# Softmax integers of a quantised cross-attention: two quarters of each row instead of one transposed by DMA, and one lag for all products with values

## The chip, the core and the metric

The kernel runs on one NeuronCore of a Trainium2 chip. The metric is the device time of one execution in microseconds (us). The core's engines each follow their own instruction queue: TensorE (PE in the profile; PEld is its weight load), VectorE (DVE), ScalarE (ACT), GpSimd (POOL) and SyncE (SP), which here only issues DMAs. All DMAs share 16 DMA engines.

## The reference, cut to what matters

The program is one layer of three parts on 512 query rows (4 x 128) of width 1024: a cross-attention to 8192 context rows, a causal self-attention, and a gated feed-forward with 4-bit weights. The change lies in the cross-attention alone:

```python
q = (x @ Wq + bq)...; k, v = (cond @ Wkv + bkv)...      # 16 heads of 64
q = _fq_sym(q, axis=-1); k = _fq_sym(k, axis=-1); v = _fq_sym(v, axis=2)
attn = softmax(einsum('bhqd,bhkd->bhqk', q, k))
attn = _fq_unsigned(attn, axis=-1)                       # round to 0..255
out = einsum('bhqk,bhkd->bhqd', attn, v)
```

Each softmax row has 8192 entries; rounded to integers 0 to 255 relative to its maximum, it is multiplied with the quantised values. TensorE contracts over partitions, so the integers, which come out with queries on partitions, must be transposed to have keys on partitions before that product.

## The kernel before, in words

Keys and values are first projected, quantised and written to DRAM (0 to about 1510 us). Then comes the attention stage (about 1513 to 2196 us), in which the change acts, then the output projection and the rest of the layer.

In the attention stage a **unit** is one head `h` and one tile `t` of 128 queries: 16 x 4 = 64 units. A unit has NSC = 8 **steps** `g` of SC = 1024 keys; four quarters `c` of KC = 2048 keys hold two steps each. A loop over `s` (line 882, inside a manual schedule, so that instructions stay on each engine in the order written) is a software pipeline:

- step `s` = 8n + g: `scores(n, g)`: two matmuls into the PSUM tile `sc` (2 buffers, line 761), then one custom VectorE instruction (line 768) that multiplies by the key scales, writes `e` (3 buffers, half a row each) and takes a running maximum `mx`. After g = 7 `maximum(n)` (lines 783, 785) makes the bias `m`.
- one unit later, at its steps 0 and 4: `exponentials` (line 796), the two halves of the row on ScalarE, written as int16 integers `a` (3 buffers).
- LAG_T = 12 steps after the scores: `transposes(n, g)` (lines 811 to 816): pairs of 16-bit integers are taken as one 32-bit word, four TensorE transposes of 128 x 128 words go to the PSUM tile `a_pt` (3 buffers), and one copy brings them to `aT` in SBUF (6 buffers). The copy is ScalarE's, but VectorE's for g = COPY_DVE = 4.
- quarter DMA_KC = 1 (g = 2 and 3) is transposed by one DMA from SyncE instead (`dma_transposes`, line 825), issued at step 4 of the next unit, into `aT_d` (2 buffers). TensorE's word transposes take even and odd keys apart and the DMA does not, so the order in which keys are stored depends on the quarter (`in_order`, line 571, used by `store_k` and `key_scales`).
- LAG_V = 16 steps after the scores (LAG_D = 20 for the quarter that the DMA transposes): `values(n, g)` (line 839): eight matmuls of 64 columns into the PSUM tile `av`, which holds the four units of a head and has one buffer. After the head's last product VectorE scales it into `xo` (lines 851 to 862).
- in a head's last unit (t = 3) SyncE loads the next head's keys `kt` (line 615, four DMAs) and GpSimd broadcasts its key scales (line 741); GpSimd's queue also loads the values `vq` (line 731, four DMAs for each pair of heads, 5 buffers) at given steps.

Of the kernel before, what the change touches and what calls it, by code (L numbers as in the profile page):

```python
# [36 lines left out]
F16 = mybir.dt.float16  # L37
I32 = mybir.dt.int32
# [8 lines left out]
P = 128  # L47
# [4 lines left out]
NP = H // 2  # L52
# [3 lines left out]
KC = 2048  # L56
NKC = NK // KC
SC = 1024
NSC = NK // SC
NEC = 2  # L60
EC = NK // NEC
LAG_T = NSC + 4
LAG_V = NSC + 8
COPY_DVE = 4
DMA_KC = 1
LAG_D = NSC + 12
INNER = 2816
WORDS = INNER // 8
V_AUTO = KT - 4
# [17 lines left out]
def tile_perceiver(  # L87
# [26 lines left out]
    nc = tc.nc  # L114
# [338 lines left out]
    for t, at in enumerate((4, 10.5, 20, 22.6)):  # L453
# [3 lines left out]
        for n in range(2):  # L457
            at = (10 + 8.15 * t, 42.6 + 7.05 * t)[n]
# [16 lines left out]
    at = 70.8  # L475
# [95 lines left out]
    def in_order(t, c):  # L571

        dims = "p h" if len(t.shape) == 3 else "p"
        if c == DMA_KC:
            return t.rearrange(f"{dims} (e n) -> {dims} n e", e=2)
        return t.rearrange(f"{dims} (n e) -> {dims} n e", e=2)

# [35 lines left out]
    def load_keys(h, c):  # L613
        kt = pools["keys"].tile([P, KC // 2], BF16, name=f"kt{h}_{c}", tag="kt", bufs=6)
        nc.sync.dma_start(out=kt, in_=k_d[c][h].rearrange("f d n -> (f d) n"))
        kts[h, c] = kt
# [5 lines left out]
    def load_scales(h, g):  # L622
        c, half = divmod(g, 2)
        nc.sync.dma_start(
            out=tile_of_scales(h, g), in_=sk_d[c][h, ts(half, SC)].partition_broadcast(P)
        )
# [4 lines left out]
    for s in range(V_AUTO, 2 * KT):  # L631
        at = TILE * s
# [8 lines left out]
    at = TILE * V_AUTO  # L641
# [11 lines left out]
    at = TILE * (KT - 2)  # L653
# [5 lines left out]
    at = TILE * KT  # L659
# [12 lines left out]
    for u in range(KT):  # L672
        at = TILE * (KT + u)
        s = KT + u
# [14 lines left out]
    at = TILE * (KT + 2)  # L689
# [4 lines left out]
    first, last = V_QUANT  # L694
    done = 0
    for u in range(first, last):
        at = TILE * (KT + u)
# [5 lines left out]
    at = TILE * (2 * KT - 1)  # L703
# [17 lines left out]
    with tc.tile_pool(name="at_s", bufs=4) as small, tc.tile_pool(  # L721
        name="at", bufs=2
    ) as at, tc.tile_pool(name="sc_ps", bufs=2, space=PSUM) as sc_ps, tc.tile_pool(
        name="at_ps", bufs=3, space=PSUM
# [3 lines left out]
        def load_values(p, c):  # L728

            vqs[p, c] = at.tile([P, KT // NKC, P], F16, name=f"vq{p}_{c}", tag="vq", bufs=NKC + 1)  # L730
            nc.gpsimd.dma_start(out=vqs[p, c], in_=vq_d[p, :, ts(c, KT // NKC), :])

        def load_rows(h):

            sks_at[h] = at.tile([P, KC], F32, name=f"sk_row{h}", tag="sk_row", bufs=1)
            for c in range(NKC):
                nc.gpsimd.dma_start(out=sks_at[h][32 * c : 32 * c + 1, :], in_=sk_d[c][h : h + 1, :])
# [7 lines left out]
        units = [(h, t) for h in range(H) for t in range(NT)]  # L745
        state, avs, sums = {}, {}, {}
# [44 lines left out]
        def exponentials(n, c):  # L791
            h, t = units[n]
            st = state[n]
            a = at.tile([P, EC], I16, name="a", tag="a", bufs=3)
            st["a"].append(a)
            nc.scalar.activation(  # L796
                a,
                st["e"][c],
                AF.Exp,
                bias=st["m"],  # L800
                scale=sq[:, t, h : h + 1],
                accum_out=sums[h][:, t, c : c + 1],
            )

        def transposes(n, g):

            a = state[n]["a"][g // (NSC // NEC)].bitcast(F32)
            at_word = SC // 2 * (g % (NSC // NEC))
            pt = at_ps.tile([P, SC // 256, P], F32, name="a_pt", tag="a_pt")
            for i in range(SC // 256):  # L810
                nc.tensor.transpose(  # L811
                    pt[:, i, :], a[:, at_word + P * i : at_word + P * i + P], ident
                )
            aT = at.tile([P, SC // 256, P], I32, name="aT", tag="aT", bufs=6)
            copy = nc.vector.tensor_copy if g == COPY_DVE else nc.scalar.copy
            copy(aT, pt.bitcast(I32))  # L816
            aT = aT.bitcast(F16).rearrange("p i (q e) -> p i e q", e=2)
            state[n]["aT", g] = [aT[:, i // 2, i % 2, :] for i in range(SC // P)]

        def dma_transposes(n):  # L820

            at_key = DMA_KC * KC % EC
            a = state[n]["a"][DMA_KC * KC // EC][:, at_key : at_key + KC].bitcast(F16)
            aT = at.tile([P, KC // P, P], F16, name="aT_d", tag="aT_d")
            nc.sync.dma_start_transpose(out=aT, in_=a)
            for g in range(KC // SC):
                state[n]["aT", KC // SC * DMA_KC + g] = [
                    aT[:, g * (SC // P) + i, :] for i in range(SC // P)
                ]

        def values(n, g):
            h, t = units[n]
            p, j = divmod(h, 2)
            if t == 0 and g == 0:
                avs[h] = at_ps.tile([P, NT, D], F32, name="av", tag="av", bufs=1)
            last = g == KC // SC * (DMA_KC + 1) - 1
            for i, aT in enumerate(state[n].pop(("aT", g))):
                c, k = divmod(g * (SC // P) + i, KT // NKC)
                nc.tensor.matmul(  # L839
                    avs[h][:, t, :],  # L840
                    lhsT=aT,
                    rhs=vqs[p, c][:, k, ts(j, D)],
                    start=(g == 0 and i == 0),
                    stop=(last and i == SC // P - 1),
                )
            if not last:
                return
            del state[n]
            if t == NT - 1:
                r = small.tile([P, NT], F32, name="r", tag="r")  # L850
                nc.vector.tensor_reduce(r, sums[h], AX.X, ALU.add)
                nc.vector.reciprocal(r, r)
                o = xo[h // 8][:, :, ts(h % 8, D)]
                nc.vector.scalar_tensor_tensor(  # L854
                    o,
                    avs[h],
                    F16_UNITS,
                    sv[:, ts(h, D)].unsqueeze(1).to_broadcast([P, NT, D]),
                    ALU.mult,
                    ALU.mult,  # L860
                )
                nc.vector.tensor_tensor(
                    o, o, r.unsqueeze(2).to_broadcast([P, NT, D]), ALU.mult
                )
# [2 lines left out]
        load_keys(0, NKC - 1)  # L867
        for g in range(NSC - 2, NSC):
            load_scales(0, g)

        order = [c for c in range(NKC) if c != DMA_KC] + [DMA_KC]
        load_rows(1)
        nc.sync.dma_start(out=sv, in_=sv_d[0].partition_broadcast(P))
        nc.sync.dma_start(out=bp, in_=xbp.partition_broadcast(P))
# [1 line left out]
        n_steps = len(units) * NSC  # L876

        def at_step(s):
            return divmod(s, NSC) if 0 <= s < n_steps else None

        with tc.manual_schedule():
            for s in range(n_steps + LAG_D):
                n, g = divmod(s, NSC)
                if s == 1:
                    for c in order:
                        load_values(0, c)
                if g == NSC // NEC and 1 <= n <= len(units):
                    dma_transposes(n - 1)
                if g % (NSC // NEC) == 0 and 1 <= n <= len(units):
                    exponentials(n - 1, g // (NSC // NEC))  # L890
                if n < len(units):
                    h, t = units[n]
                    scores(n, g)
                    if t == NT - 1 and h + 1 < H:

                        if g < NKC:
                            load_keys(h + 1, g)
                        spread_scales(h + 1, g)
                        if g == NSC - 1 and h + 2 < H:
                            load_rows(h + 2)  # L900
                    if g == NSC - 1:
                        maximum(n)
                for lag, work, dma in (
                    (LAG_T, transposes, False),
                    (LAG_V, values, False),
                    (LAG_D, values, True),
                ):
                    at_lag = at_step(s - lag)
                    if at_lag and (at_lag[1] * SC // KC == DMA_KC) == dma:
                        work(*at_lag)  # L910

                pair, since = divmod(s - NSC * (2 * NT - 1), NSC * 2 * NT)
                if 0 <= pair < NP - 1 and since in (0, LAG_V + 1, LAG_V + 5, LAG_V + 7):
                    load_values(pair + 1, order[(0, LAG_V + 1, LAG_V + 5, LAG_V + 7).index(since)])


    xq.close()
# [287 lines left out]
    with tc.manual_schedule():  # L1205
# [11 lines left out]
        for h, (w, n) in enumerate(PARTS):  # L1217
            s = PART * h

            if h > 0:  # L1220
                for kp in range(NC // 2):
                    at = s + {1: (-28, -22, -16, -10), 2: (-37, -33, -6, -3)}.get(h, (-26, -16, -6, -3))[kp]
# [15 lines left out]
            for t in range(NT):  # L1238
                g = s + GROUP * t
# [42 lines left out]
        s = PART * len(PARTS)  # L1282
        for i in range(2):
            at = s - 26 + 10 * i
# [9 lines left out]
    with tc.tile_pool(name="ff_t", bufs=2) as ff_t, tc.tile_pool(name="ff", bufs=1) as ff:  # L1294
# [63 lines left out]
        with tc.tile_pool(name="ff_h", bufs=1) as ff_h, tc.tile_pool(  # L1358
            name="y_ps", bufs=1, space=PSUM
        ) as y_ps:  # L1360
            y = ff_h.tile([P, NT, C], F32, name="y")
            for n in range(2):
# [4 lines left out]
                for q in range(NI // 2):  # L1367
# [5 lines left out]
                    for t in range(NT):  # L1373
                        for j in (2 * q, 2 * q + 1):
                            for i, ps in enumerate((yab[t][0], yab[t][0], yab[t][1])):
# [5 lines left out]
                                    stop=(j == NI - 1 and i != 0),  # L1381
# [91 lines left out]
```

## Time and profile before

| | |
|---|---|
| median of 3 runs | 2919.16 us (2917.12 to 2919.83) |
| the profiled execution, its own time | 2917.71 us |
| its span, first to last instruction | 2915.9 us |
| granted TensorE clock over the span | 0.985 |
| PE busy over the span | 2714.9 us (93%) |
| DVE busy | 2447.8 us (84%) |
| ACT busy | 1308.2 us (45%) |
| line 768 on DVE (512 instructions) | 595.1 us, first at 1513.4, last at 2181.1 us |
| line 796 on ACT (128) | 487.4 us |
| line 816 on ACT (320) and on DVE (64) | 168.4 us; 682 to 691 ns each on DVE |

Shares over the whole span mix stages: TensorE fills the projection before and much of the layer behind, so the attention stage must be read by itself. In the profile, "busy" adds up instructions of an engine, "idle before" is the engine's wait, and the name behind the arrow is what ended the wait. Two instructions that follow each other on an engine overlap a little in the records, so the cost of one in a row is best read as the distance between two starts.

### The profile page before, as it was taken

Reading aid. Unit: us, or ns where it says so; the run is one execution under the profiler, and the core shown is the slowest. Engines: PE = TensorE matmul, PEld = TensorE weight load, DVE = VectorE, ACT = ScalarE, POOL = GpSimd, SP = SyncE. Lnnn points to the kernel's source line nnn. Section 1 sums busy time; section 2 is a strip of 40 time slices with the busy share of each in tenths; the row PEclk is TensorE's granted clock in tenths of the full one; section 3 lists DMA queues with packets and bytes.
Section 4 is the critical chain, followed back from the end, with each engine's and each line's share of the span. In section 5 each row is a group of like instructions: output and inputs, shape, how many; then the busy total and the mean of one; then the engine's idle time right before and its main releaser. Section 6 shows DMA issues by size and latency. Waiting matters only on the chain.

```text
span 2915.9 us, 42024 instructions
## 1 busy us (share of the span) xinstructions
PE 2714.9 (93%) x15992; PEld 2103.4 (72%) x15992; DVE 2447.8 (84%) x4010; ACT 1308.2 (45%) x1473; POOL 442.0 (15%) x596
## 2 busy tenths in 40 slices
PE   8999999999999999999978888888878899799998
PEld 3788888888888888888845555555555677688876
DVE  6899998555799888989769999999995898676674
ACT  4212121111323333333229999999994244333332
POOL 0011111000022222222113223322311000000000
PEclk9999999999999999999979999999999999899999
DMA  5555565222457777776354445444433221122222
GB/s 184 179 199 195 197 214 196 99 89 101 145 132 199 195 183 195 185 189 177 98 164 90 104 94 108 109 107 99 95 81 128 87 77 58 51 94 94 94 87 94
DMA packets 321226, 383.83 MB, mean 132 GB/s; under 512 B 224064, under 2 KB 228736, under 8 KB 321024
## 3 DMA queue, kind: packets, MB, share of 16 engines
q1 hardware_dynamic: 274528, 227.02, 28.9%
q0 software_dynamic: 45440, 153.09, 16.3%
q8 instruction: 125, 2.05, 0.3%
q10 hardware_dynamic: 1056, 1.05, 0.2%
q14 instruction: 77, 0.63, 0.1%
HBM read 224.30 MB, written 104.34 MB: 113 GB/s over the span
## 4 chain that ended last, share of the span: by engine, by line
PE 69%; DVE 16%; issue 8%; ACT 5%; DMA 1%; POOL 0%; SPq 0%; DVEq 0%; ACTq 0%; POOLq 0%
PE kv_a L344 32%; PE kv_b L344 16%; DVE e L768 10%; PE y_a L1376 3%; PE gate_a L165 3%; PE up_a L165 3%; PE acc_a L1031 3%; ACT aT L816 2%; ACT a L796 2%; PE q_ps L293 2%; PE y_b L1376 1%; PE gate_b L165 1%; PE up_b L165 1%; PE acc_b L1031 1%; PE a_pt L811 1%
## 5 line engine op out<-in xcount | busy, mean ns | idle before, releaser
L344 PE MATMUL kv_a<-w_h,c_h 128*128 128x512 f32 x2048 | 806.4, 394 | 0.0
L344 PE MATMUL kv_a<-w_l,c_l 128*128 128x512 f32 x2048 | 806.0, 394 | 0.2 <-ACT w_l L247 0.2
L344 PE MATMUL kv_b<-w_d,c_d 128*128 128x512 f32 x2048 | 805.9, 394 | 0.0
L768 DVE CUSTOM_DVE_ANT_0 e<-sc,sk 128x1024 f32<-128x1024 f32 x512 | 595.1, 1218 | 13.1 <-DMA kt<-k_d 11.4
L796 ACT ACTIVATE a<-e,m,sq 128x4096 int16<-128x4096 f32 x128 | 487.4, 3808 | 19.4 <-DVE m L785 14.2
L344 PEld LDWEIGHTS kv_a<-w_l,c_l 128*128 128x128 f32 x2048 | 384.8, 188 | 89.6 <-ACT w_l L247 0.6
L344 PEld LDWEIGHTS kv_a<-w_h,c_h 128*128 128x128 f32 x2048 | 384.8, 188 | 88.9 <-issue 0.2
L344 PEld LDWEIGHTS kv_b<-w_d,c_d 128*128 128x128 f32 x2048 | 384.8, 188 | 88.9 <-DVE c_d L159 0.2
L155 ACT ACTIVATE c_h<-c_raw 128x1024 fp32r<-128x1024 f32 x128 | 135.1, 1056 | 422.5 <-PE kv_a L344 412.7
L358 DVE SCALAR_TENSOR_TENSOR f<-kv_a,bkv 128x512 f32<-128x512 f32 x256 | 175.6, 686 | 164.3 <-PE kv_a L344 163.6
L761 PE MATMUL sc<-kt,qT 64*128 64x512 bf16 x1024 | 204.0, 390 | 107.2 <-DVE mx L768 98.7
L811 PE MATMUL a_pt<-ident,a 128*128 128x128 f32 x1536 | 253.9, 288 | 13.0 <-ACT a L796 7.9
L811 PEld LDWEIGHTS a_pt<-ident,a 128*128 128x128 f32 x1536 | 162.6, 142 | 104.2 <-issue 49.7
L583 ACT CAST kst<-kT 128x512 bf16<-128x512 int16 x128 | 94.5, 738 | 301.2 <-DMA kT<-ki 301.1
L741 POOL PARTITION_BROADCAST sk<-sk_row x120 | 143.2, 1297 | 332.7 <-DVE mx L768 332.3
L359 DVE SCALAR_TENSOR_TENSOR f<-kv_b,f 128x512 f32<-128x512 f32 x256 | 176.6, 690 | 20.0 <-DVE f L358 1.4
L761 PEld LDWEIGHTS <-qT 64*128 64x128 bf16 x1024 | 76.6, 93 | 148.8 <-issue 106.7
L816 ACT COPY aT<-a_pt 128x512 int32<-128x512 int32 x320 | 168.4, 586 | 3.8 <-PE a_pt L811 3.6
L158 DVE TENSOR_TENSOR fw_l<-fw_raw,fw_h 128x1024 fp32r<-128x1024 f32 x64 | 78.2, 1223 | 107.1 <-ACT fw_h L155 107.0
L839 PE MATMUL av<-vq,aT 128*128 128x64 f16 x3072 | 154.3, 194 | 14.4 <-DVE xo L854 14.4
L839 PEld LDWEIGHTS <-aT 128*128 128x128 f16 x3072 | 130.2, 99 | 49.0 <-issue 43.8
L158 DVE TENSOR_TENSOR c_l<-c_raw,c_h 128x1024 fp32r<-128x1024 f32 x128 | 155.6, 1216 | 4.9 <-ACT c_h L155 4.1
(190 smaller groups left out, 3998.1 us busy)
## 6 DMA issues: line engine op xcount, KB each, us to landing
c_raw<-in_ctxT SPq DMA_DIRECT2D x128, 512.0 KB, 3.8
v_d<-f POOLq DMA_DIRECT2D x64, 512.0 KB, 3.1
vl<-v_d POOLq DMA_DIRECT2D x64, 512.0 KB, 4.2
gu_d<-w_ffn POOLq DMA_DIRECT2D x44, 512.0 KB, 3.1
fw_raw<-gu_d SPq DMA_DIRECT2D x42, 512.0 KB, 3.2
k_d<-kst POOLq DMA_DIRECT2D x128, 128.0 KB, 3.5
vq_d<-vq POOLq DMA_DIRECT2D x32, 512.0 KB, 4.9
kt<-k_d SPq DMA_DIRECT2D x64, 256.0 KB, 3.3
```

What stands on the lines that cost most here:

```text
L158: nc.vector.tensor_tensor(lo, src, hi, ALU.subtract)
L165: nc.tensor.matmul(ps, lhsT=lhs(i, k), rhs=rhs(i, k), start=(k == 0 and i != 1), stop=(k == NC - 1 and i != 0),)
L344: nc.tensor.matmul(ps, lhsT=tokens[s][i][:, k, :], rhs=w3[s < KT][k][i][:, ts(n, 512)], start=(k == 0 and i != 1), stop=(k == NC - 1 and i ...
L358: nc.vector.scalar_tensor_tensor(f, a, 1.0 + 1.0 / UP, bias[s < KT][n], ALU.mult, ALU.add)
L359: nc.vector.scalar_tensor_tensor(f, b, -1.0 / UP, f, ALU.mult, ALU.add)
L741: nc.gpsimd.partition_broadcast(tile_of_scales(h, g), sks_at[h][32 * c : 32 * c + 1, ts(half, SC)], channels=P)
L761: nc.tensor.matmul(ps[:, ts(i, 512)], lhsT=qT[rows, h, ts(t, P)], rhs=kts[h, g // 2][rows, ts(g % 2, 512)], start=True, stop=True,)
L768: nc.vector.tensor_tensor_reduce(out=state[n]["e"][-1][:, ts(g % (NSC // NEC), SC)], in0=ps, in1=sks_at[h, g], scale=1.0, scalar=LOWEST, o ...
L796: nc.scalar.activation(a, st["e"][c], AF.Exp, bias=st["m"], scale=sq[:, t, h : h + 1], accum_out=sums[h][:, t, c : c + 1],)
L811: nc.tensor.transpose(pt[:, i, :], a[:, at_word + P * i : at_word + P * i + P], ident)
L816: copy(aT, pt.bitcast(I32))
L839: nc.tensor.matmul(avs[h][:, t, :], lhsT=aT, rhs=vqs[p, c][:, k, ts(j, D)], start=(g == 0 and i == 0), stop=(last and i == SC // P - 1),)
```

## The change

A second quarter, c = 3 (g = 6 and 7), is transposed by DMA, issued at step 0 of the unit after the next. TensorE then transposes g = 0, 1, 4 and 5 only, and all their copies are ScalarE's. All products with values follow 18 steps behind the scores. `aT` has 4 buffers, `aT_d` 3. The keys of quarter 3 are stored in the order of the DMA's quarters. Values are loaded in natural order, at other steps.

```diff
-LAG_V = NSC + 8
-COPY_DVE = 4
-DMA_KC = 1
-LAG_D = NSC + 12
+LAG_V = NSC + 10
+DMA_KC = (1, 3)
...
-        if c == DMA_KC:
+        if c in DMA_KC:
...
-            aT = at.tile([P, SC // 256, P], I32, name="aT", tag="aT", bufs=6)
-            copy = nc.vector.tensor_copy if g == COPY_DVE else nc.scalar.copy
-            copy(aT, pt.bitcast(I32))
+            aT = at.tile([P, SC // 256, P], I32, name="aT", tag="aT", bufs=4)
+            nc.scalar.copy(aT, pt.bitcast(I32))
...
-        def dma_transposes(n):
+        def dma_transposes(n, c):
...
-            aT = at.tile([P, KC // P, P], F16, name="aT_d", tag="aT_d")
+            aT = at.tile([P, KC // P, P], F16, name="aT_d", tag="aT_d", bufs=3)
             nc.sync.dma_start_transpose(out=aT, in_=a)
...
-            last = g == KC // SC * (DMA_KC + 1) - 1
...
-                    stop=(last and i == SC // P - 1),
+                    stop=(g == NSC - 1 and i == SC // P - 1),
...
-            if not last:
+            if g < NSC - 1:
...
-                    for c in order:
+                    for c in range(NKC):
                         load_values(0, c)
                 if g == NSC // NEC and 1 <= n <= len(units):
-                    dma_transposes(n - 1)
+                    dma_transposes(n - 1, DMA_KC[0])
+                if g == 0 and 2 <= n <= len(units) + 1:
+                    dma_transposes(n - 2, DMA_KC[1])
...
-                for lag, work, dma in (
-                    (LAG_T, transposes, False),
-                    (LAG_V, values, False),
-                    (LAG_D, values, True),
-                ):
-                    at_lag = at_step(s - lag)
-                    if at_lag and (at_lag[1] * SC // KC == DMA_KC) == dma:
-                        work(*at_lag)
+                at_lag = at_step(s - LAG_T)
+                if at_lag and at_lag[1] * SC // KC not in DMA_KC:
+                    transposes(*at_lag)
+                if at_step(s - LAG_V):
+                    values(*at_step(s - LAG_V))
...
-                if 0 <= pair < NP - 1 and since in (0, LAG_V + 1, LAG_V + 5, LAG_V + 7):
-                    load_values(pair + 1, order[(0, LAG_V + 1, LAG_V + 5, LAG_V + 7).index(since)])
+                if 0 <= pair < NP - 1 and since in (0, LAG_V + 1, LAG_V + 3, LAG_V + 5):
+                    load_values(pair + 1, max(0, since - LAG_V + 1) // 2)
```

More of the change, by code (lines that the diff above doesn't have):

```diff
@@ L813, in transposes @@
                 )
-            aT = at.tile([P, SC // 256, P], I32, name="aT", tag="aT", bufs=6)
-            copy = nc.vector.tensor_copy if g == COPY_DVE else nc.scalar.copy
-            copy(aT, pt.bitcast(I32))
+            aT = at.tile([P, SC // 256, P], I32, name="aT", tag="aT", bufs=4)
+            nc.scalar.copy(aT, pt.bitcast(I32))
             aT = aT.bitcast(F16).rearrange("p i (q e) -> p i e q", e=2)
             state[n]["aT", g] = [aT[:, i // 2, i % 2, :] for i in range(SC // P)]
-        def dma_transposes(n):
-            at_key = DMA_KC * KC % EC
-            a = state[n]["a"][DMA_KC * KC // EC][:, at_key : at_key + KC].bitcast(F16)
-            aT = at.tile([P, KC // P, P], F16, name="aT_d", tag="aT_d")
+        def dma_transposes(n, c):
+            at_key = c * KC % EC
+            a = state[n]["a"][c * KC // EC][:, at_key : at_key + KC].bitcast(F16)
+            aT = at.tile([P, KC // P, P], F16, name="aT_d", tag="aT_d", bufs=3)
             nc.sync.dma_start_transpose(out=aT, in_=a)
             for g in range(KC // SC):
-                state[n]["aT", KC // SC * DMA_KC + g] = [
+                state[n]["aT", KC // SC * c + g] = [
                     aT[:, g * (SC // P) + i, :] for i in range(SC // P)
@@ L869, in tile_perceiver @@
             load_scales(0, g)
-        order = [c for c in range(NKC) if c != DMA_KC] + [DMA_KC]
         load_rows(1)
@@ L881, in tile_perceiver @@
         with tc.manual_schedule():
-            for s in range(n_steps + LAG_D):
+            for s in range(n_steps + LAG_V):
                 n, g = divmod(s, NSC)
                 if s == 1:
-                    for c in order:
+                    for c in range(NKC):
                         load_values(0, c)
                 if g == NSC // NEC and 1 <= n <= len(units):
-                    dma_transposes(n - 1)
+                    dma_transposes(n - 1, DMA_KC[0])
+                if g == 0 and 2 <= n <= len(units) + 1:
+                    dma_transposes(n - 2, DMA_KC[1])
                 if g % (NSC // NEC) == 0 and 1 <= n <= len(units):
```

## Prediction, made before the changed kernel ran

> **What bounds the kernel now.** The page gives PE 93% of the span and DVE 84%, but the change acts only while line 768 runs, so I first read the busy time of each engine in stretches of that stage (columns: PE, weight loads, DVE, ACT, POOL busy, clock, DMA share, GB/s).
>
> ```profile
> 1700.00:1800.00 100.00, 81.94 (x975) 57.97 (x976) 99.09 (x195) 96.07 (x86) 27.92 (x31) 1.00 0.47 108
> 1800.00:1900.00 100.00, 83.50 (x1016) 59.02 (x1015) 99.16 (x192) 97.05 (x88) 34.08 (x39) 1.00 0.46 99
> 1900.00:2000.00 100.00, 82.05 (x973) 57.85 (x972) 99.16 (x192) 96.88 (x87) 25.00 (x28) 1.00 0.42 93
> ```
>
> Here VectorE is the bound (99% busy), ScalarE is close (97%), PE has 17% and DMA more than half to spare. Next, the timeline of one unit, for what VectorE's period is made of and how far ScalarE is from it (columns: start, duration, engine, line, operation; in brackets idle time).
>
> ```profile
> 1806.04 1.22 DVE L768 CUSTOM_DVE_ANT_0 e<-sc,sk 128x1024 f32<-128x1024 f32 x1
> 1806.14 3.80 ACT L796 ACTIVATE a<-e,m,sq 128x4096 int16<-128x4096 f32 x1
> ...
> 1807.19 0.69 DVE L816 COPY aT<-a_pt 128x512 int32<-128x512 int32 x1
> ...
> 1807.80 1.21 DVE L768 CUSTOM_DVE_ANT_0 e<-sc,sk 128x1024 f32<-128x1024 f32 x1
> ...
> 1808.94 1.22 DVE L768 CUSTOM_DVE_ANT_0 e<-sc,sk 128x1024 f32<-128x1024 f32 x1
> ...
> 1809.95 1.54 ACT L816 COPY aT<-a_pt 128x512 int32<-128x512 int32 x3
> ...
> 1811.37 3.82 ACT L796 ACTIVATE a<-e,m,sq 128x4096 int16<-128x4096 f32 x1
> ...
> 1815.16 1.07 ACT L816 COPY aT<-a_pt 128x512 int32<-128x512 int32 x2
> ...
> 1816.12 0.21 DVE L785 TENSOR_SCALAR m<-m,nsq 128x1 f32<-128x1 f32 x1
> ...
> 1816.25 1.21 DVE L768 CUSTOM_DVE_ANT_0 e<-sc,sk 128x1024 f32<-128x1024 f32 x1
> ...
> 1816.36 3.80 ACT L796 ACTIVATE a<-e,m,sq 128x4096 int16<-128x4096 f32 x1
> ```
>
> The period is 1816.25 - 1806.04 = 10.21 us: eight line-768 instructions about 1.145 us apart (9.16), a copy, and the maximum (0.45). With the copy between them two line-768 starts are 1.76 us apart here, 1.74 in the next unit: the copy costs **0.60 us**. ScalarE: exponential to copies 3.81 and 3.79 us, three copies to the next exponential 1.42, two copies about 0.95 (they end at 1816.23, and the other exponential overlapped its copies by 0.12), so a copy costs 0.47 and the unit needs 9.97 us; for the rest it waits for `m`. Last, the DMA transposes, by their tile (issue on SyncE in ns, min/median/max, then issue to landing):
>
> ```profile
> L825 SPq DMA_TRANSPOSE aT_d<-a x64: 1665/1983/3858, 1528.5 to 2186.7; - x64
> ...
> DMA to landing us min/median/max: 4.2/4.4/6.9
> ```
>
> **The change, part by part.**
>
> *VectorE's copy goes.* 64 copies; those of the last two units start at 2182.68 and 2192.68, behind the last line-768 instruction (2181.09), so 62 lie on the bounding engine: 62 x 0.60 = **-37.2 us**. The unit becomes 9.61 us.
>
> *What is late next: ScalarE.* It makes five copies now (g = 0, 1, 5, 6, 7) and four after, two behind each exponential: 2 x (3.80 + 0.95) = 9.50 us, 0.11 under VectorE. Cost 0, with little cover. Above: priced by their full 586 ns, four copies and two exponentials of 3.80 make 9.94, and the gain shrinks to 0.27 us a unit (rival B). Below: nothing, since VectorE is behind it. VectorE's step 4 reuses the `e` buffer that the first exponential frees: that ends about 4.0 us into the unit, step 4 begins at 4 x 1.145 = 4.58, so 0.5 us cover.
>
> *TensorE* loses two of six groups of four transposes a unit (0.66 us busy each). It is not the bound: 0 gain. Its copies are due no sooner: products move from 16 to 18 steps for g = 0, 1, 4 to 7, which is 2.3 us more room; for g = 2, 3 from 20 to 18. The copies of g = 0, 1 end at the unit's end and are read two steps later. Four `aT` buffers fit four tiles a unit, read six steps after their transposes and rewritten after eight. Cost 0.
>
> *A second DMA transpose a unit.* In the trace it is seen at quarter-microsecond resolution, with nothing beside it, from about 1821.4 to 1824.2 us: a DMA share of 0.9 to 1.2, in all 2.9 us of the 16 engines for 512 KB. Four units take 41.85 us (first scale broadcasts of two heads, 1839.00 and 1880.85), so 10.46 a unit on average, of which DMA is busy 0.455 x 10.46 = 4.8 us. After: 7.7 of about 9.9 us, 77%: it fits. Waits on SyncE: the transpose of quarter 1 waits for the first exponential (4.0 us into the unit), that of quarter 3 for the second (about 8.7 us, a microsecond before the step at which it is written), so they alternate 4.7 and 4.9 us apart, each about 2 us of issue. Behind them queue the next head's four `kt` loads, held back by up to 2 us of issue, with 9 us until their first use and 3.4 us to land. Deadlines of the transposes: products eight steps after the step of issue, at least 9.2 us; and the exponential that rewrites the source buffer, one unit and about a microsecond after the issue. Landing takes 4.4 us, at worst 6.9. Cost 0; what is queued behind a late one is ScalarE's exponential, and behind that VectorE (rival C). Of the three `aT_d` buffers each is free about three steps before its next use.
>
> [...]
>
> *Values' loads* move to steps 19, 21, 23 and are needed at 28, 30, 32: 10 us for 3.8 (at worst 6.8) to land. GpSimd waits longer for `av`, with no broadcast behind it until step 32. *Key order of quarter 3*: its ScalarE casts (line 583) take 0.62 instead of 0.78 us, as quarter 1's do; ScalarE waited 301 us for its transposes there. Both 0.
>
> *Scaling of a head's output* (lines 851 to 862) moves from behind the maximum to behind step 1. It delays line 768 by 1.04 us now; then PE has finished the last product about 1 us earlier, so no wait; the extra gap in the row of line-768 instructions costs 0 to 0.1 us, taken 0.1 x 15 = **+1.5 us**. PE's next product waits for it until about 3.2 us into the unit, its scores for step 3 are ready at 3.9 and used at 4.5.
>
> *The end of the stage.* Before: bias ready at 2182.76, first scaling of the last head at 2195.95, 13.2 us. After: first exponential +3.9, two copies instead of three, second exponential done at about +8.7, then the DMA transpose of quarter 3, 4.4 to land (bounds 4.2 and 6.9), and 16 products, 0.8: about 14.0. **+0.8 us** (bounds 0.6 and 3.3).
>
> Sum: -37.2 + 1.5 + 0.8 = -34.9 us. The profiled execution's 2917.7 us (span 2915.9 and 1.8 around it) becomes 2882.8; the median of the runs is 1.5 us above it: **2884 us**.
>
> **The rivals.**
>
> *A, the forecast*, 0.68. VectorE stays the bound. From 2876 (the two costs vanish, and VectorE's remaining idle time of 0.85% of 668 us mostly with them) to 2892 (the tail at 3.3, ScalarE's bound 0.1 us higher a unit).
>
> *B, ScalarE becomes the bound*, 0.12. By the full durations above: 62 x 0.27 = 17 us less gain on top of the two costs: about 2905. For it: 97% busy, 0.11 us of cover. Against it: the starts, which give 0.47 a copy in both groups.
>
> *C, slower: transfers on SyncE's queue do not overlap.* 0.12. If each kept the queue from issue to landing, a head would need 8 x 4.4 + 4 x 3.4 = 48.8 us, against 39.5 that VectorE will need and 41.85 now: +7 x 16 = 111 us, 3030 us. It decides once a head's transfers exceed 39.5 us. For it: all go through one queue, and no two of these transposes were in flight together before. Against it: the engine time is 2.9 us of the 4.4, and a `kt` of 256 KB lands in 3.4 us though the engines moved up to 397 GB/s then.
>
> *D, slower: TensorE's clock falls*, 0.03. The first units' score matmuls take 0.61 us a pair (0.39 later) with idle gaps of 0.53, so a half-busy PE stayed slow. PE is busy 83% of 10.46 = 8.7 us a unit now and (8.7 - 1.3) / 9.9 = 75% after, at full speed. [...] By the row, slow scores and transposes (1.11 us) and products 1.6 times as long (0.61 by 0.39; 0.64 us for eight, an estimate) make 8 x 0.61 + 4 x 1.11 + 8 x 0.64 = 14.4 us a unit: +270 us, about 3190. I take 0: the loss of work is small.
>
> *E, the gain is given back* by a wait between B and C, 0.05: about 2919.
>
> **How the numbers follow.** This kernel's measurement can tell about 0.2% (5.8 us) from no change. Faster: A + B = 0.80; same: E, 0.05; slower: C + D, 0.15. The range reaches from A's lower end over B and half of E to 2920 and leaves out C, D and a little else. A's own range is 2876 to 2892.
>
> **What would show it.** Right: line 816 only on ACT, 256 times; starts of line 768 even at 1.145 us, unit 9.6; DVE still near 99% in the stage; last line-768 start about 36 us earlier (near 2145); DMA share near 0.77; PE near 75% at clock 1.0. Wrong: idle time before line 768 ended by ACT (B), exponentials that wait for a DMA and landings over 9 us (C), score pairs at 0.61 us inside the stage (D), a tail over 17 us.

## The result, and the profile after

| | before | after |
|---|---|---|
| median (4 runs each) | 2918.14 us | 2889.50 us |
| range | 2916.08 to 2919.83 | 2888.83 to 2893.55 |
| profiled execution, its own time / span | 2917.71 / 2915.9 us | 2888.83 / 2887.1 us |
| first and last start of the score instruction on DVE | 1513.4, 2181.1 us | 1510.9, 2149.3 us |

The ratio is 0.9905 with a 95% interval of 0.9888 to 0.9922: 28.6 us faster by the medians, where 2884 us (34 to 35 us) was forecast. Lines 768, 796, 811, 816 and 839 of the kernel before are 766, 794, 809, 813 and 835 now.

The same three stretches of the attention stage (columns as before: PE, weight loads, DVE, ACT, POOL busy, granted clock, DMA share, GB/s):

```profile
1700.00:1800.00 100.00, 78.78 (x970) 55.20 (x970) 98.39 (x189) 95.91 (x81) 36.26 (x40) 0.98 0.83 160
1800.00:1900.00 100.00, 78.07 (x960) 54.76 (x960) 98.39 (x195) 97.72 (x84) 24.89 (x28) 0.98 0.77 149
1900.00:2000.00 100.00, 79.51 (x960) 56.06 (x960) 97.48 (x189) 94.18 (x77) 36.94 (x41) 0.97 0.82 165
```

DMA has risen to about 0.81 as expected (0.77), VectorE is still the bound. But two columns are not as forecast: VectorE fell from 99.1 to 98.1, and TensorE's clock from 1.00 to 0.98. One unit in the timeline:

```profile
1801.60 1.21 DVE L766 CUSTOM_DVE_ANT_0 e<-sc,sk 128x1024 f32<-128x1024 f32 x1
1801.72 3.80 ACT L794 ACTIVATE a<-e,m,sq 128x4096 int16<-128x4096 f32 x1
...
1802.74 1.22 DVE L766 CUSTOM_DVE_ANT_0 e<-sc,sk 128x1024 f32<-128x1024 f32 x1
...
1803.88 1.22 DVE L766 CUSTOM_DVE_ANT_0 e<-sc,sk 128x1024 f32<-128x1024 f32 x1
...
1805.52 1.05 ACT L813 COPY aT<-a_pt 128x512 int32<-128x512 int32 x2
...
1806.46 3.81 ACT L794 ACTIVATE a<-e,m,sq 128x4096 int16<-128x4096 f32 x1
...
1810.26 1.06 ACT L813 COPY aT<-a_pt 128x512 int32<-128x512 int32 x2
...
1811.19 1.21 DVE L766 CUSTOM_DVE_ANT_0 e<-sc,sk 128x1024 f32<-128x1024 f32 x1
```

The unit is 1811.19 - 1801.60 = 9.59 us, the score instructions are even at 1.14 us, and ScalarE has two copies behind each exponential: the main step of the prediction as written. A unit in which VectorE also scales a finished head is longer; the others are called plain here. The 64 units, from the first start of each to the next: 9.59 to 9.62 us for nearly all plain ones (10.19 to 10.21 before), and 10.65 us for nine of the fifteen that hold a head's scaling (11.24 before). The rest stand out: after the first three units, six units with a scaling last 11.38 to 11.58 us, and two plain ones 10.71 and 10.72. In one of the six, what happens is seen in the clock (three stretches of 5 us, then TensorE and VectorE around the middle one):

```profile
1770.00:1775.00 5.00, 3.48 (x46) 2.64 (x47) 4.86 (x13) 5.00 (x5) 0.00 (x0) 1.00 1.16 307
1775.00:1780.00 5.00, 4.57 (x40) 3.09 (x39) 4.23 (x9) 5.00 (x6) 0.00 (x0) 0.66 0.81 164
1780.00:1785.00 5.00, 3.89 (x50) 2.75 (x48) 4.93 (x11) 3.03 (x3) 1.30 (x2) 1.00 0.82 186
```

```profile
1773.82 0.39 PE L835 MATMUL av<-vq,aT 128*128 128x64 f16 x8 [1.35 <-DVE xo L850]
...
1776.42 0.64 PE L835 MATMUL av<-vq,aT_d 128*128 128x64 f16 x8
1776.98 0.61 PE L759 MATMUL sc<-kt,qT 64*128 64x512 bf16 x2
1777.52 1.11 PE L809 MATMUL a_pt<-ident,a 128*128 128x128 f32 x4
1778.43 0.63 PE L835 MATMUL av<-vq,aT_d 128*128 128x64 f16 x8
1779.00 0.60 PE L759 MATMUL sc<-kt,qT 64*128 64x512 bf16 x2
```

```profile
1777.63 1.23 DVE L766 CUSTOM_DVE_ANT_0 e<-sc,sk 128x1024 f32<-128x1024 f32 x1
...
1779.64 1.22 DVE L766 CUSTOM_DVE_ANT_0 e<-sc,sk 128x1024 f32<-128x1024 f32 x1 [0.77 <-PE sc L759]
```

For about 3.4 us TensorE runs at half clock (0.50 granted from 1776.05 to 1779.46 us): scores 0.61 instead of 0.39 us, transposes 1.11 instead of 0.66. A step with transposes then takes about 2 us (score starts 1776.98 and 1779.00), VectorE runs out of scores and waits. In the whole stage VectorE's idle time before the score instruction, ended by scores from TensorE, went from 0.8 to 6.9 us (us, times; the kernel before, then the changed one):

```profile
  PE sc L761: 0.8, 2
...
  PE sc L759: 6.9, 13
```

A stretch of some 3.4 us at half clock like this one is called a dip below. Between 1540 and 2145 us the changed kernel has eight; the kernel before had one, at 2037 us, which lengthened no unit.

The DMA transposes, by their tile:

```profile
L822 SPq DMA_TRANSPOSE aT_d<-a x128: 1678/1944/4958, 1526.0 to 2159.7; - x128
...
DMA to landing us min/median/max: 4.2/4.3/9.0
```

Twice as many, the median issue and landing much as before, only the worst cases longer.

### The profile page after: what moved, and what is told of

The parts are those of the page before. It is cut to its first block, busy times and chain, and to the rows that moved or that the text cites. A ratio compares the mean times of both kernels' runs of the same rounds, so it can differ in the third digit from the quotient of the medians.

```text
span 2887.1 us, 41022 instructions
## 1 busy us (share of the span) xinstructions
PE 2666.1 (92%) x15480; PEld 2066.9 (72%) x15480; DVE 2411.5 (84%) x3946; ACT 1271.2 (44%) x1409; POOL 444.4 (15%) x596
## 3 DMA queue, kind: packets, MB, share of 16 engines
q10 hardware_dynamic: 1056, 1.05, 0.2%
## 5 line engine op out<-in xcount | busy, mean ns | idle before, releaser
L809 PE MATMUL a_pt<-ident,a 128*128 128x128 f32 x1024 | 176.9, 298 | 22.7 <-ACT a L794 18.0
L809 PEld LDWEIGHTS a_pt<-ident,a 128*128 128x128 f32 x1024 | 112.9, 146 | 88.6 <-ACT a L794 50.6
L157 DVE SCALAR_TENSOR_TENSOR c_d<-c_l,c_raw 128x1024 fp32r<-128x1024 f32 x128 | 156.3, 1221 | 2.3
L153 ACT ACTIVATE fw_h<-fw_raw 128x1024 fp32r<-128x1024 f32 x64 | 67.7, 1060 | 179.5 <-PE y_a L1369 75.2
L548 ACT CAST vq<-vi 128x1024 f16<-128x1024 int16 x64 | 66.9, 1046 | 172.2 <-DVE vi L541 123.8
```

The source lines that it names most:

```text
L153: nc.scalar.mul(hi, src, 1.0 - 0.5 / UP)
L157: nc.vector.scalar_tensor_tensor(df, lo, -1.0 - UP, src, ALU.mult, ALU.add)
L809: nc.tensor.transpose(pt[:, i, :], a[:, at_word + P * i : at_word + P * i + P], ident)
```

## The experiments

Theory 1: the missing part of the gain is these clock dips, set off by TensorE's wait (1.35 us above) for a head's scaling. Theory 2: TensorE's lighter load itself sets them off. Theory 3: the DMA engines, 80% busy, make something late. "Idle behind scores" below is VectorE's, over the stage; dips are counted between 1540 and 2145 us.

**e1: two product tiles**, so that TensorE need not wait for the scaling.

```diff
-            pt = at_ps.tile([P, SC // 256, P], F32, name="a_pt", tag="a_pt")
+            pt = at_ps.tile([P, SC // 256, P], F32, name="a_pt", tag="a_pt", bufs=2)
-                avs[h] = at_ps.tile([P, NT, D], F32, name="av", tag="av", bufs=1)
+                avs[h] = at_ps.tile([P, NT, D], F32, name="av", tag="av", bufs=2)
```

> The changed kernel with two buffers for the product tile of a head (and, to make room in PSUM, two instead of three for the transposes), so that TensorE no longer waits about 1.35 us for the scaling of the head before. Theory 1 (the missing 6 us of the gain are stretches of about 3.5 us in which TensorE's clock is halved, set off by that wait among light steps): no clock dips inside the stage, idle time of line 766 behind scores falls from 6.9 us to about 1.2 us (that of the first steps), about 5.5 us faster than the changed kernel, 2884 us. Theory 2 (the dips come from TensorE's lower load as a whole): the dips stay, within 1.5 us of 2889.5. Theory 3 (the 80% busy DMA engines make something late): within 1.5 us as well, with the waits still there.

**e2: the control**, the first of the two edits alone.

> The control for the run before: the changed kernel with two instead of three buffers for the transposes alone. TensorE can then wait for ScalarE's copies once a unit. All theories: VectorE has about 0.5 us of cover, so within 3 us of 2889.5, with the clock dips still there; if it is faster by 5 us, the buffers and not the wait for the scaling explain the run before.

Measured: e1 2906.2 us (ratio to before 0.995, 0.9934 to 0.9967), e2 2903.8 us (0.9951, 0.9936 to 0.9965). They are some 17 and 14 us slower than the changed kernel, so e2's own expectation failed: two buffers for the transposes are not free. TensorE's transposes wait for ScalarE's copies, and most plain units become 9.67 to 9.78 us:

```profile
PEld a_pt L809 <- ACT aT L813: 53.6, 65, 1.0
...
PE a_pt L809 <- ACT aT L813: 34.3, 57, 0.7
```

(e2, waits between 1700 and 2100 us: total us, times, longest; the changed kernel has 14.0 us of the first between 1690 and 2080 and the second not at all.) For the question at hand the pair is still of use: with the wait for the scaling (e2) there are fourteen dips and idle behind scores is 14.9 us, without it (e1) twelve and 13.3 us, in a profile that caught e1's fastest run. Removing the wait brought no time. Theory 1 in this form falls: while VectorE scales for a microsecond it takes no scores, and in e1 TensorE's longest wait for it to free a score buffer is 1.5 us instead of 0.5, so TensorE is short of work anyway.

**e3: more work for TensorE.** The scores of steps 2 and 3, in which it has no transposes, are done twice; the result is the same.

```diff
-            for i in range(2):
+            for i in (0, 1, 0, 1) if g in (2, 3) else (0, 1):
```

> The changed kernel, in which the two score matmuls of steps 2 and 3 of every unit are done twice (same result, 128 x 2 matmul pairs more, about 0.33 us of TensorE each), in the very steps that are light. Theories 1 and 2 (clock): more work on TensorE, yet fewer or no dips, about 4 to 6 us faster than the changed kernel, 2884 us. Theory 3 (DMA): no gain; the scores take 0.33 us more where they are late, so 0 to 3 us slower.

Measured: 2883.6 us (2880.4 to 2884.8), ratio 0.9877 (0.9862 to 0.9892). It does more, moves the same bytes, and is faster by about 6 us than the changed kernel, whose four runs lie at 2888.8 to 2893.6. In the profiles, first to last score instruction takes 633.2 us instead of 638.4. Two dips are left; thirteen of the fifteen units with a scaling last 10.64 to 10.66 us, and idle behind scores is 2.6 us. A stretch without a dip (the first below; the second has one) has the clock and VectorE's 99% back, at nearly the same DMA share:

```profile
1700.00:1800.00 100.00, 82.24 (x1018) 55.20 (x1015) 99.12 (x193) 96.83 (x84) 36.20 (x40) 1.00 0.80 160
1800.00:1900.00 100.00, 82.61 (x1009) 55.56 (x1007) 98.35 (x193) 96.32 (x81) 24.85 (x28) 0.98 0.78 150
```

So the clock is the cause; theory 3 does not explain a gain from extra matmuls.

**e4: the lag alone** on the kernel before (one quarter by DMA, the copy still on VectorE).

```diff
-LAG_V = NSC + 8
-LAG_D = NSC + 12
+LAG_V = NSC + 10
+LAG_D = NSC + 10
...
-            last = g == KC // SC * (DMA_KC + 1) - 1
+            last = g == NSC - 1
...
-        order = [c for c in range(NKC) if c != DMA_KC] + [DMA_KC]
+        order = list(range(NKC))
```

(and values loaded at steps 0, 19, 21, 23, as in the change)

> The kernel before with the lag part of the change alone: all products at 18 steps, values loaded in natural order at the new steps, one quarter transposed by DMA, the copy of g = 4 still on VectorE. The prediction's sum: +1.5 us for the scaling between two line-768 instructions, the tail shorter or equal: 2919 to 2921 us. Theory 1: dips need the wait among light steps; with two more groups of transposes in the unit (steps 2 and 3 too) there are none or few: 2920. If the lag alone costs 5 us or more, the shortfall belongs to the lag and not to the lighter TensorE.

Measured: 2923.4 us, ratio 1.0013 (1.0006 to 1.0020), so 2 to 6 us slower. In its profile the unit with a scaling lasts 11.24 to 11.26 us, as before: the scaling between two score instructions costs nothing. Two such units have a dip and last 12.04, and first to last score instruction takes 1.8 us more than before (669.4 against 667.7). With more transposes on TensorE dips are rare, but not absent. By the profile, then, the lag alone brings two costly dips and the whole change eight; by the times alone, 4 us could be most of the shortfall. e9 below takes the lag back to 16 steps in the changed kernel and gains nothing clear (2888.2 against 2889.5 us), which speaks for the lighter load. What makes up the rest of e4's 4 us is open; in its profile it lies behind the last score instruction (739.3 against 734.8 us to the end).

**e5: the copy of g = 4 back on VectorE**, in the changed kernel.

```diff
-            nc.scalar.copy(aT, pt.bitcast(I32))
+            copy = nc.vector.tensor_copy if g == 4 else nc.scalar.copy
+            copy(aT, pt.bitcast(I32))
```

> The changed kernel with one of its four copies, that of g = 4, put back on VectorE. If the gain is VectorE's copy, the unit goes from 9.61 back to 10.21 us: 62 x 0.60 = +37 us on 2889.5, and since TensorE then does the smaller work in the longer unit, more clock dips: 2926 to 2933 us, slower than the kernel before. If the gain came from fewer TensorE transposes or from ScalarE, less than 15 us of it would go: under 2905.

Measured: 2941.3 us, ratio 1.0072 (1.0057 to 1.0087): slower than the kernel before, and 8 us above the expected range. The plain unit without a dip is 10.19 to 10.21 us again, so the copy is worth its 37 us. The surplus is the clock: with the smaller TensorE work in the longer unit, all fifteen units with a scaling have a dip. Ten of them last 12.02 to 12.17 us and five 11.37 to 11.40 (11.24 before); behind the ten the next unit most often has a dip as well. Idle behind scores is 17.7 us:

```profile
1700.00:1800.00 100.00, 75.50 (x888) 52.79 (x884) 97.16 (x188) 85.72 (x67) 26.86 (x31) 0.93 0.75 154
1800.00:1900.00 100.00, 76.88 (x889) 53.99 (x888) 95.78 (x184) 84.04 (x67) 32.63 (x34) 0.91 0.74 154
```

PE's busy share looks hardly lower than in the changed kernel because slow matmuls count for longer; the clock column tells them apart.

**e6: ScalarE's cover.** The copy of g = 0 is done twice.

```diff
-            nc.scalar.copy(aT, pt.bitcast(I32))
+            for _ in range(2 if g == 0 else 1):
+                nc.scalar.copy(aT, pt.bitcast(I32))
```

> The changed kernel with the copy of g = 0 done twice on ScalarE (same result), to measure how much cover ScalarE has. With 0.47 us a copy ScalarE needs 9.97 us a unit against VectorE's 9.61; it falls behind by 0.36 us a unit, of which about 0.58 is covered before step 4 waits for it, and the unit with the scaling (10.65) lets it catch up: about 0.5 us a head, +7 us, 2897. With the 586 ns of the records a copy it would be 10.09 a unit and about 0.9 us a head: +13 us, 2903. If ScalarE had more cover than the prediction said: under 2891.

Measured: 2903.9 us (2899.4 to 2906.8), ratio 0.9953 (0.9936 to 0.9969). In most heads the plain units are now about 9.61, 9.82 and 10.02 us instead of 9.61 thrice (in five of the early ones the second is 10.22): 0.62 us a head, between the two prices given, together with idle behind scores up from 6.9 to 9.6 us and eleven dips. ScalarE is 99% busy:

```profile
1700.00:1800.00 100.00, 76.07 (x946) 52.78 (x943) 97.04 (x187) 99.26 (x87) 36.26 (x40) 0.98 0.82 165
```

So ScalarE stands close behind VectorE, as the 0.11 us of cover said: one more copy, 0.47 us, is felt. How large the cover is to a tenth, the run doesn't tell.

**e7: three quarters by DMA**, TensorE transposes g = 4 and 5 only.

```diff
-DMA_KC = (1, 3)
+DMA_KC = (0, 1, 3)
...
-                    dma_transposes(n - 1, DMA_KC[0])
+                    for c in DMA_KC[:2]:
+                        dma_transposes(n - 1, c)
...
-                    dma_transposes(n - 2, DMA_KC[1])
+                    dma_transposes(n - 2, DMA_KC[2])
```

(`aT` with 2 buffers, `aT_d` with 4)

> The changed kernel with quarter 0 transposed by DMA too, three a unit, only quarter 2 by TensorE, two buffers for its copies and four for the DMA's. VectorE's work is the same. If the DMA engines are bound by the 2.9 us that one transpose takes of them, a unit needs 3 x 2.9 + 1.9 = 10.6 us on average against 9.87: about +0.7 us a unit, +45 us, 2935. If they have room left (their recorded share can exceed 1), the unit stays at 9.61 and only TensorE's lighter load shows, with more dips: +5 to +25 us, 2895 to 2915.

Measured: 2916.2 us (2908.6 to 2925.7), ratio 0.9993 (0.9982 to 1.0004). The whole gain is gone, yet 19 us less than a full DMA bound would cost. The profile, of a run 7 us above the median, shows two causes (the transposes' tile, then waits between 1700 and 2100 us):

```profile
L822 SPq DMA_TRANSPOSE aT_d<-a x192: 1692/2558/9253, 1526.0 to 2196.8; - x192
...
DMA to landing us min/median/max: 4.2/5.1/13.9
```

```profile
PEld L835 <- DMA aT_d<-a: 29.8, 16, 7.0
DVE e L766 <- PE sc L759: 23.9, 26, 6.0
PE av L835 <- DMA aT_d<-a: 23.6, 11, 6.7
ACT a L794 <- DMA aT_d<-a: 20.6, 7, 6.7
```

Many units are still 9.6 us, others up to 17: transposes land up to 13.9 us after their issue, TensorE's products and ScalarE's exponentials wait for them, and the clock is at 0.86. How much is late transfers and how much the clock is not told apart here. Late transfers cost time at this DMA share, 1.06 to 1.11; at the changed kernel's 0.81 no product or exponential waits for one between 1540 and 2145 us, and no run lies between.

**e8: the extra work only behind a scaling** (units t = 2, the scores of step 2 thrice and of step 3 twice).

```diff
-            for i in range(2):
+            times = {2: 3, 3: 2}.get(g, 1) if t == 2 else 1
+            for i in times * [0, 1]:
```

> The changed kernel with extra TensorE work only where the dips begin: in the units in which a head is scaled (t = 2), the score matmuls of step 2 are done three times and those of step 3 twice (same result, about 1 us of TensorE a head). If the dips are TensorE's light stretch around VectorE's scaling: no dips between 1540 and 2145 us, every such unit 10.65 us, 6 us faster than the changed kernel: 2883. If the average load decides, this adds 2.5% of it and the dips stay: 2888 to 2890.

Measured: 2884.9 us (2881.5 to 2888.6), ratio 0.9884 (0.987 to 0.9899). Every unit with a scaling is 10.65 to 10.67 us now, as expected, but four plain units behind one last 10.69 to 10.74: five dips are left of eight, four of them in these units, so some are gone and some have moved on by one unit. Idle behind scores is 6.0 us against 6.9, so its profile explains little of the 4.6 us by which the median is lower. Its medium result stands between the two theories: the stretch behind the scaling is the lightest one, not the only light one.

**e9: products at 16 steps**, which puts the scaling behind the maximum and in front of two steps with transposes.

```diff
-LAG_V = NSC + 10
+LAG_V = NSC + 8
```

> The changed kernel with products 16 steps behind the scores instead of 18. VectorE's scaling of a head then comes behind the maximum, as in the kernel before, and the steps that follow it (0 and 1) have TensorE transposes. If the place of the scaling ahead of two light steps sets off the dips, most go: 2884 us. If TensorE's load alone does it, they stay: 2889 us. Against it: the products of quarter 3 follow six steps (6.9 us) behind the issue of its DMA transpose, which landed in 4.3 us in the median and 9.0 at worst, and those of g = 0 and 1 follow ScalarE's copies closely; waits there would make TensorE idle, bring more dips, and 2890 to 2905 us.

Measured: 2888.2 us (2884.1 to 2891.2), ratio 0.9887 (0.9869 to 0.9904): no different from the changed kernel. Nine dips, but in other units and for 4.8 us of idle behind scores; the units with a scaling are all 10.64 to 10.66. The place of the scaling decides where dips fall and what each costs, not whether they come. The feared waits for DMA transposes are there and small (6.0 us of weight loads in 400 us).

**e10: scores twice in all four light steps** (2, 3, 6 and 7).

```diff
-            for i in range(2):
+            for i in (0, 1, 0, 1) if g in (2, 3, 6, 7) else (0, 1):
```

> The changed kernel with the score matmuls done twice in all four light steps (2, 3, 6 and 7), about 1.3 us of TensorE a unit that serves nothing. If the dips come from TensorE's light stretches, the two that were left with steps 2 and 3 alone go as well: 2882 us, no dip between 1540 and 2145 us. TensorE's step is then about 1.05 us of 1.145: if that makes scores late, 2890 us or more.

Measured: 2883.6 us (2881.9 to 2886.3), ratio 0.9876 (0.9860 to 0.9891), the same as e3. Four dips remain, at every third head from 1695 us on, each in a unit with a scaling, and each costs 1.14 us now (11.79 against 10.65), probably because the extra scores are slow as well. The expectation of no dip failed, and filling further does not pay.

e3 and e10 beat both kernels: 1.2% below the kernel before. That they beat the changed one rests on separate medians (about 6 us); the intervals of the ratios overlap slightly.

## Why the prediction was right, point by point

**The copy off VectorE: right.** -0.60 us a unit was forecast; plain units went from 10.20 to 9.60, those with a scaling from 11.24 to 10.65. e5 puts the copy back and gets 10.20 again. Rival B did not come: with four copies no unit waits for ScalarE, and with a fifth, in e6, some do. (Rival B's "17 us less gain" is a slip of words: 62 x 0.27 is the gain that would be left. Its 2905 us follows from that.)

**The second DMA transpose at no cost in transfers: right.** 77% of the DMA engines was forecast, 0.81 is the mean of the three stretches. Median landing stayed at 4.3 us, at worst 9.0 instead of 6.9, just inside the deadline of 9.2. What it did cost came through TensorE's lighter load, below. Rival C did not come: transfers do overlap, since a head's transfers by its price would have needed 48.8 us and the head took about 39.5.

**The scaling's place, +1.5 us: wrong in size.** It costs nothing more: the excess over a plain unit is 1.05 us (10.65 - 9.60), 1.04 before.

**The tail, +0.8 us: right.** From the last head's bias (2150.99) to its scaling (2164.90) 13.9 us, 13.2 before: +0.7.

**TensorE's clock at no cost: the step that failed.** The prediction wrote "I take 0: the loss of work is small". By the lengths of the units, eight dips cost 7.4 us. The prediction compared mean loads, 83% before and 75% after, and knew only two outcomes, no fall or a lasting one at +270 us; in the runs the clock falls for 3.4 us at a time, at about 0.9 us each. That a lighter load would leave the clock alone no trace had shown, and its own row, in which a half-busy TensorE stayed slow (0.61 us a pair with gaps of 0.53), spoke against it. In the 3.5 us ahead of the dip at 1776 us the longest gap was 1.35 us and TensorE was busy 0.18 + 0.50 + 0.38 + 0.07 + 0.50 = 1.63 us, 47%: the clock halved behind light work, with no longer pause in it. Yet the stretch behind the scaling at 1813 us is as light (1.74 of 3.5 us) and has no dip. The places of the dips tell the two apart. The eight dips begin at 1615.62, 1625.86, 1656.58, 1776.05, 1895.52, 1905.76, 1936.48 and 2055.94 us, that is 3, 9, 35, 35, 3, 9 and 35 times 3.413 us apart. In the profiles of both kernels, e3 and e5 to e10 all changes of the clock between 1540 and 2145 us fit one such grid each, whose offset from the start of the span lay between 0.08 us (e8) and 3.34 us (e5). On the grid the two stretches are not alike (columns as above):

```profile
1772.64:1776.05 3.41, 1.68 (x23) 1.14 (x23) 3.35 (x9) 3.41 (x5) 0.00 (x0) 1.00 1.19 244
1776.05:1779.46 3.41, 3.41 (x28) 2.31 (x26) 2.82 (x6) 3.41 (x2) 0.00 (x0) 0.50 0.83 158
...
1810.18:1813.60 3.41, 2.42 (x28) 1.89 (x29) 3.34 (x9) 3.41 (x5) 0.00 (x0) 1.00 0.67 127
1813.60:1817.01 3.41, 2.26 (x34) 1.66 (x33) 3.34 (x9) 3.41 (x5) 0.00 (x0) 1.00 0.33 63
```

The first stretch fills one window, in which TensorE is 49% busy, and the clock is halved in the next. The second is split between two windows of 71% and 66%, and nothing happens. In the changed kernel's profile, of the full-clock windows of the grid between 1540 and 2145 us, the six with TensorE 45 to 55% busy were all followed by a dip, two of the nine at 58 to 62% were, and none above was; in the kernel before, one at 62% was, and others at 61 and 62% were not. At about 60%, then, busy time in these profiles does not decide. So a short light stretch mattered here, not the mean, and of the two equally light ones above the grid tells the one that was hit.

**What was luck.** The measured 2889.5 us lies inside the forecast's own range of 2876 to 2892, but the upper end was made for a longer tail and a slower ScalarE. The dips fell into that room, and the scaling's 1.5 us, charged for nothing, covered a part of them.

**The sum.** -37.2 for the copies, +7.4 for dips, +0.2 for one early unit give -29.6; first to last score instruction shows 667.7 to 638.4, -29.3. The stage began 2.5 us earlier, and after it the program took 3.0 us longer (737.8 against 734.8 from the last score instruction), 0.7 of it the tail. In all the profiles here the start lies between 1509.9 and 1515.4 us and that rest between 734 and 739 us, with no relation to the edits, so these two are taken as scatter. -29.3 - 2.5 + 3.0 = -28.8, the change of the span.

## What to carry to other kernels

When an edit takes work off the bounding engine and off TensorE together, look for its lightest stretch of some 3.4 us and at the granted clock there, not at means: here TensorE, about 79% busy in the stage and not its bound, made VectorE wait when its clock halved, and its busy share rose from 49% in one window of 3.41 us to 100% in the next. Read the cost of a copy from the distance of two starts, and the next bound from the same timeline. The second transpose by DMA was worth its price here, where the two engines that copy from PSUM were 99% and 97% busy and the DMA share was 0.42 to 0.47 before; count that share first, since with a third transpose, at 1.06 to 1.11 (e7), the whole gain was gone, by late transfers and more dips together.

## What the runs showed of the hardware that was not expected

- In the attention stage the changes of TensorE's clock lay on a grid of 3.413 us (1615.62, 1625.86, 1656.58 us and so on in the changed kernel), and it halved behind windows in which TensorE was 45 to 62% busy there, with no gap above 1.35 us; adding useless matmuls (an estimated 0.66 us a unit, from 0.33 a pair) took 6 us off the kernel (e3: 2883.6 against 2889.5 us).
- In the first steps of the stage TensorE stayed at half clock from 1503 to 1537 us in the changed kernel (to 1532 in the kernel before), though the score matmuls came every 1.14 us and took 0.61 of it.
- Two PSUM buffers instead of three for the transposes cost 14 us; 8 us of it is VectorE's idle time behind scores (14.9 against 6.9), with fourteen dips instead of eight.
